# Layer 1 attention: the last key blocks of two query sets transposed together in every second slot, and the adjacency diagonal treated on GpSimd

## The chip, the cores and the metric

The kernel runs on one core of one Trainium2 chip. The metric is the device time of one execution in microseconds (us). TensorE is called PE here (its weight loads PEld), VectorE DVE, ScalarE ACT, GpSimd POOL, and SyncE, which issues the transfers, SP. All data is float32.

## The reference

Two graph layers over 4096 nodes with 512 features, each behind a layer norm and a Relu, each added to its input. The change touches the second layer alone:

```python
# --- layer 1 ---
h = jnp.maximum(_layernorm(x, axis=-1), 0.0)
adj = jnp.maximum(adjacency, jnp.eye(4096))          # 4096 x 4096
keys    = jnp.einsum('nj,hjk->hnk', h, Wks)          # 8 heads of 64
queries = jnp.einsum('nj,hjk->hnk', h, Wqs)
values  = jnp.einsum('nj,hjk->hnk', h, Wvs)
atts = jnp.einsum('hqk,hmk->hqm', queries, keys) / 8
atts = atts - 1e16 * (1.0 - adj)[None, :, :]
atts = softmax(atts, axis=-1)
x = x + jnp.einsum('hqm,hmk,hko->qo', atts, values, Wo)
```

The adjacency holds zeros, values of up to 1e9, and a diagonal.

## The kernel before, in words

Layer 0 comes first, and writes its output, the queries, keys and values of layer 1 to DRAM. Layer 1 starts about halfway through the span.

Layer 1 works on pairs of heads (`c` = 0 to 3). For each pair it goes through 128 **sets** of 32 query rows. A set is folded so that it fills all partitions: partition quadrant `a` (32 partitions) holds the 32 queries against keys `a*1024` to `a*1024+1023`, so a set is a tile of 128 x 1024 for each of the two heads. Four sets make a group (128 queries). The exponentials live in a ring `t` of 12 sets.

One loop runs over **slots** `s`, one set per slot, 512 slots and a few more. In one slot, sets of different age are at different stages. The order of instructions on every engine is the order of the program text; no scheduler moves them. The stages of a slot, in that order:

- `with_self(s+1)` (L897): for pair 0 alone, DVE takes the maximum of the set's 32x32 diagonal block of the adjacency and the identity. The block is in partition quadrant 0 for sets 0 to 31, quadrant 1 for sets 32 to 63, and so on.
- `keep_penalty(s)` (L906): for pair 0, SP writes the finished penalty to DRAM, from where the pairs 1 to 3 load it again (L886).
- `squares(s-4)` (L973): DVE transposes the first 768 key columns of both heads in blocks of 32x32, in place.
- `turned(s-4)` (L979): PE transposes the last 256 key columns, two 128x128 blocks for each head, into the PSUM tile `tr`.
- `smallest` (L950, L955), in odd slots: a matmul `nmB` and a DVE reduction give the softmax shift `nm` of the two sets `s-3` and `s-2`.
- `scores(s)` (L915) and `masked(s)` (L931): PE multiplies queries and keys into four PSUM tiles `sc` (tiles of 64 rows by 32 columns of the array), and DVE adds the penalty `a` and keeps the minimum, in four pieces.
- `taken(s-4)` (L985): ACT copies `tr` back into `t`.
- `exps(s-3)` (L966): ACT's two exponentials.
- `made_penalty(s+1)` (L901, L902): for pair 0, ACT's Relu on the adjacency tile and POOL's `(a - 1) * -1e16`.
- `parted(s)` (L940), in odd slots: POOL prepares the operand of `nmB`.
- `weighted(s-8)` (L996): PE multiplies values by exponentials (tiles of 128 rows by 64 columns of the array), a quarter of the keys of a whole group in each slot. The last quarter reads what `turned` gave.
- `divided`: now and then a sum over partitions (`tot`, L1011), a reciprocal and a small transpose (`invT`, L1019) for half a pair of heads.
- `prefetch(s+5)`: SP's loads of the adjacency (pair 0: four transfers of 128 KB, L889) or of the penalty (L886).

PSUM has eight banks: `sc` takes four, `tr` one, `nmB`, `tot` and `invT` share two (pool `a1m`), and `o` one.

Of the kernel before, what the change touches and what calls it, by code (L numbers as in the profile page):

```python
# [8 lines left out]
F32 = mybir.dt.float32  # L9
AF = mybir.ActivationFunctionType  # L10
ALU = mybir.AluOpType
AX = mybir.AxisListType
PSUM = bass.MemoryType.PSUM
DRAM = bass.MemoryType.DRAM

P = 128
# [7 lines left out]
def kernel(  # L24
# [14 lines left out]
    nc = tc.nc  # L39
# [14 lines left out]
    ident = const.tile([P, P], F32, name="ident")  # L54
# [5 lines left out]
    SQ = 32  # L60
# [38 lines left out]
    with tc.tile_pool(name="a0k", bufs=1) as pk, tc.tile_pool(name="a0v", bufs=4) as pv, tc.tile_pool(  # L99
        name="a0a", bufs=3  # L100
    ) as pa, tc.tile_pool(name="a0t", bufs=6) as pt, tc.tile_pool(name="a0p", bufs=4) as pp, tc.tile_pool(
        name="a0x", bufs=1
    ) as px, tc.tile_pool(name="a0h", bufs=3) as ph, tc.tile_pool(name="a0s", bufs=4) as psb, tc.tile_pool(
        name="a0tr", bufs=3, space=PSUM
# [68 lines left out]
        def turned(G, i):  # L173

            trs = []
            for b in range(MB):
                if b % 4 == 0:
                    tr = ptr.tile([P, TW], F32, name="tr")
                    trs.append(tr)
                for h in range(2):  # L180
                    nc.tensor.transpose(  # L181
                        tr[:, bass.ts(b % 4 * 2 + h, P)], G.t[h][:, bass.ts(i * MB + b, P)], ident
                    )
            return trs

        def taken(G, i, trs):
            for j, tr in enumerate(trs):
                pT = pp.tile([P, TW], F32, name="pT")
                if tiles_out[0] % 7 in (2, 5):
                    nc.scalar.copy(pT, tr)  # L190
                else:
                    nc.vector.tensor_copy(pT, tr)  # L192
                tiles_out[0] += 1
                G.pT[i, j] = pT
# [230 lines left out]
        def step(n):  # L425
            return groups[n // 2], n % 2

        with tc.manual_schedule():
# [45 lines left out]
            for s in range(total + 6):  # L474
                G, h = step(s) if s < total else (None, 0)
                for half in range(2):
# [4 lines left out]
                    turn = 0 <= n < 2 * total  # L481
# [11 lines left out]
                    if half == 1 and s + 1 < total:  # L493
                        leaky(*step(s + 1))

                        c, at = divmod(s + 3, 2 * NB)
# [11 lines left out]
                    if 1 <= n <= 2 * total:  # L508
                        W, w = groups[(n - 1) // HALVES], (n - 1) % HALVES
# [12 lines left out]
    QK_ = N // NS  # L522
    GS = P // SQ
# [4 lines left out]
    EXPS, TURN, PROD = 3, 4, 8  # L528
    BR = 2
    UNITS = 6  # L530
    with tc.tile_pool(name="b0c", bufs=1) as pc, tc.tile_pool(name="b0a", bufs=4) as pa, tc.tile_pool(
        name="b0w", bufs=1
    ) as pk, tc.tile_pool(name="b0t", bufs=1) as pt, tc.tile_pool(name="b0v", bufs=GS) as pv, tc.tile_pool(
        name="b0x", bufs=6
    ) as pxr, tc.tile_pool(name="b0h", bufs=4) as ph, tc.tile_pool(name="b0e", bufs=4) as pe, tc.tile_pool(
        name="b0ht", bufs=2
    ) as phT, tc.tile_pool(
        name="b0s", bufs=6
    ) as psb, tc.tile_pool(name="b0o", bufs=1) as px, tc.tile_pool(
        name="b0lk", bufs=2, space=PSUM  # L540
    ) as plk, tc.tile_pool(name="b0m", bufs=1, space=PSUM) as pm, tc.tile_pool(
        name="b0po", bufs=1, space=PSUM
    ) as po, tc.tile_pool(name="b0q", bufs=2, space=PSUM) as pmm:
        t = pt.tile([P, RING, 2, QK_], F32, name="bt")
# [101 lines left out]
        def squares(G, k):  # L646
            u = t[:, G.ring + k].rearrange("p h (n j) -> p h n j", j=SQ)
            nc.vector.transpose(u, u)  # L648
# [116 lines left out]
        with tc.manual_schedule():  # L765
# [4 lines left out]
            for s in range(SETS + PROD + 10):  # L770
# [23 lines left out]
                if s % 2 and s < SETS:  # L794
                    G, k = step(s)
# [3 lines left out]
                if s % 2 == 0 and 0 <= s - 2 < SETS:  # L799
                    G, k = step(s - 2)  # L800
# [3 lines left out]
                if 0 <= n < SETS:  # L804
                    W, w = step(n)
# [20 lines left out]
    VC = 768  # L826
    NV = VC // SQ
    NT = (QK_ - VC) // P
    SG = NG // 2
    with tc.tile_pool(name="a1t", bufs=1) as pt, tc.tile_pool(name="a1k", bufs=4) as pkk, tc.tile_pool(  # L830
        name="a1v", bufs=GS
    ) as pv, tc.tile_pool(name="a1a", bufs=6) as pa, tc.tile_pool(name="a1q", bufs=2) as pq, tc.tile_pool(
        name="a1x", bufs=2
    ) as px, tc.tile_pool(name="a1s", bufs=6) as psb, tc.tile_pool(name="a1z", bufs=2) as pz, tc.tile_pool(name="a1at", bufs=3) as pat, tc.tile_pool(
        name="a1sc", bufs=4, space=PSUM
    ) as psc, tc.tile_pool(name="a1tr", bufs=1, space=PSUM) as ptr, tc.tile_pool(
        name="a1m", bufs=2, space=PSUM
    ) as pm, tc.tile_pool(name="a1o", bufs=1, space=PSUM) as po:
        t = pt.tile([P, RING, 2, QK_], F32, name="t")
        sums = pt.tile([P, HC, 2, 2, SG, GS], F32, name="sums")  # L840
# [13 lines left out]
        def load_keys(c):  # L854
            keys[c] = []
            for half in range(2):
                k = pkk.tile([P, NS, HF], F32, name="k")
                nc.sync.dma_start(
                    k, qk_d[:, c, 0, :].rearrange("p (a f x) -> p f a x", a=NS, f=2)[:, half]
                )  # L860
                keys[c].append(k)
# [19 lines left out]
        def penalty(G, k):  # L881

            w = G.g * GS + k
            a = pa.tile([P, QK_], F32, name="a")
            if G.c > 0:
                nc.sync.dma_start(a, pen_d[w])  # L886
                return a
            for b in range(NS):
                nc.sync.dma_start(a[bass.ts(b, SQ)], adj[bass.ts(w, SQ), bass.ts(b, QK_)])  # L889
            return a  # L890

        def with_self(G, k, a):
            if G.c == 0:
                w = G.g * GS + k
                b, at = divmod(w * SQ, QK_)
                diag = a[bass.ts(b, SQ), bass.ds(at, SQ)]
                nc.vector.tensor_max(diag, diag, ident[bass.ts(b, SQ), bass.ts(b, SQ)])  # L897

        def made_penalty(G, k, a):
            if G.c == 0:  # L900
                nc.scalar.activation(a, a, AF.Relu)  # L901
                nc.gpsimd.tensor_scalar(a, a, -1.0, -BIG, ALU.add, ALU.mult)  # L902

        def keep_penalty(G, k, a):
# [68 lines left out]
            nc.vector.transpose(u, u)  # L973

        def turned(G, k):
            tr = ptr.tile([P, 512], F32, name="tr")
            for h in range(2):
                for m in range(NT):
                    nc.tensor.transpose(  # L979
                        tr[:, bass.ts(h * NT + m, P)], t[:, G.ring + k, h, bass.ds(VC + m * P, P)], ident  # L980
                    )
            return tr

        def taken(G, k, tr):
            nc.scalar.copy(t[:, G.ring + k, :, VC:], tr.rearrange("p (h x) -> p h x", h=2))  # L985

        def weighted(G, i):
            if i == 0:
# [102 lines left out]
        def load_queries(i):  # L1091
            q = pq.tile([P, QG * P], F32, name="q")
            c, g = divmod(i * QG, NG)
            nc.sync.dma_start(q, qk_d[:, c, 1, bass.ds(g * P, QG * P)])
            for j in range(QG):
                groups[i * QG + j].q, groups[i * QG + j].q0 = q, j * P
# [4 lines left out]
        with tc.manual_schedule():  # L1101
            pens = {}

            def prefetch(n):
                if n < total:
                    if n % (QG * GS) == 0:
                        load_queries(n // (QG * GS))
                    pens[n] = penalty(*step(n))

            AHEAD = 5  # L1110
            rb = 0
            divisions = []
            load_keys(0)
            for n in range(AHEAD):
                prefetch(n)
            with_self(*step(0), pens[0])
            made_penalty(*step(0), pens[0])
            for i in range(GS):
                load_values(0, i)
            for s in range(total + PROD + 3):  # L1120
                if s + 1 < total:
                    with_self(*step(s + 1), pens[s + 1])
                if s < total:
                    keep_penalty(*step(s), pens[s])

                c, at = divmod(s + 4, SETS)
                if 0 < c < HC and at == 0:
                    load_keys(c)
                c, at = divmod(s - PROD - 1 + GS, SETS)
                if 0 < c < HC and at < GS:  # L1130
                    load_values(c, at)
                turn = 0 <= s - TURN < total
                if turn:
                    squares(*step(s - TURN))
                    tr = turned(*step(s - TURN))

                if s % 2 and 0 <= s - 3 < total:
                    G, k = step(s - 3)
                    smallest(G, k // 2)
                n = s - PROD  # L1140
                if 0 < n <= total and n % GS == 0:
                    finish(groups[n // GS - 1])
                if s > total:
                    projected(rb)
                    rb += 1
                if s < total:
                    scs = scores(*step(s))
                    masked(*step(s), scs, pens.pop(s))
                if turn:
                    taken(*step(s - TURN), tr)  # L1150
                if 0 <= s - EXPS < total:
                    exps(*step(s - EXPS))
                if s + 1 < total:
                    made_penalty(*step(s + 1), pens[s + 1])
                if s % 2 and s < total:
                    G, k = step(s)
                    parted(G, k // 2)
                if 0 <= n < total:
                    W, w = step(n)
                    weighted(W, w)  # L1160
                if n > 1 and n % (SG * GS) == 1:
                    divisions.append(divided(*divmod(n // (SG * GS) - 1, 2)))
                for d in divisions[:1]:
                    if next(d, d) is d:
                        divisions.pop(0)
                if s == (HC - 1) * SETS + SETS // 2:
                    wot = pkk.tile([P, HC, DM], F32, tag="k", name="wot")
                    nc.sync.dma_start(wot, wo.rearrange("h d o -> (h d) o").rearrange("(c p) o -> p c o", p=P))
                if s > total - AHEAD and len(chunks) < 3:
                    load_chunk()  # L1170
                prefetch(s + AHEAD)

            for j in range(rb, NB):
                projected(j)
# [28 lines left out]
```

## Time and profile before

| | us |
|---|---|
| median of three runs | 4974.71 (4970.81 to 4975.93) |
| the profiled execution | 4974.76 |
| its span, first to last instruction | 4973.0 |
| L915 PE scores, 16384 instructions | busy 1004.0 |
| L996 PE weighted sums, 16384 | busy 1008.3 |
| L979 PE transposes, 2048 | busy 348.5 |
| L931 DVE masked pieces, 2048 | busy 1291.3 |
| L973 DVE block transposes, 512 | busy 907.7 |
| L966 ACT exponentials, 1024 | busy 1168.0 |
| L985 ACT copies of `tr`, 512 | busy 298.9 |

The span is the profiler's first to last instruction of one execution; the execution's own time is a little more. Busy times of a line add up the time in which at least one of its instructions ran. In listings by time the columns are the start, the length, the engine and line, the operation, what it writes and reads, the shapes, the count, and in brackets how long the engine had been idle before and what released it. A matmul of the program counts as two instructions there for `sc`, `o` and `nmB`, and as one for a transpose. The ends of matmuls are modelled, so two rows of PE can overlap by some hundredths of a us; the chain of waits cuts such overlaps away.

### The profile page before, as it was taken

Reading aid. Unit: us, or ns where it says so; the run is one execution under the profiler, and the core shown is the slowest. Engines: PE = TensorE matmul, PEld = TensorE weight load, DVE = VectorE, ACT = ScalarE, POOL = GpSimd, SP = SyncE. Lnnn points to the kernel's source line nnn. Section 1 sums busy time; section 2 is a strip of 40 time slices with the busy share of each in tenths; the row PEclk is TensorE's granted clock in tenths of the full one; section 3 lists DMA queues with packets and bytes.
Section 4 is the critical chain, followed back from the end, with each engine's and each line's share of the span. In section 5 each row is a group of like instructions: output and inputs, shape, how many; then the busy total and the mean of one; then the engine's idle time right before and its main releaser. Section 6 shows DMA issues by size and latency. Waiting matters only on the chain.

```text
span 4973.0 us, 145263 instructions
## 1 busy us (share of the span) xinstructions
PE 4747.3 (95%) x61554; PEld 3507.7 (71%) x61554; DVE 4509.1 (91%) x7969; ACT 3912.2 (79%) x4557; POOL 396.1 (8%) x676
## 2 busy tenths in 40 slices
PE   6999999999999868998989999999999999999998
PEld 5888888888888756776746656666666666666664
DVE  4999999999999898888659999999999999999981
ACT  4999999999999898888658888666666666666660
POOL 1000000000000011111112222000000000000000
PEclk8999999999999979999999999999999999999999
DMA  6444454445444474444377787634444343533435
GB/s 236 156 150 162 171 183 154 157 154 197 165 147 163 121 170 141 134 143 141 100 217 242 239 261 239 200 129 144 137 160 152 128 153 127 187 128 136 152 121 191
DMA packets 358842, 819.49 MB, mean 165 GB/s; under 512 B 60080, under 2 KB 179120, under 8 KB 333104
## 3 DMA queue, kind: packets, MB, share of 16 engines
q1 hardware_dynamic: 358192, 810.21, 49.8%
q8 instruction: 483, 7.91, 0.7%
q14 instruction: 167, 1.37, 0.1%
HBM read 669.26 MB, written 140.77 MB: 163 GB/s over the span
## 4 chain that ended last, share of the span: by engine, by line
PE 42%; DMA 3%; issue 2%; SPq 1%; ACT 1%; DVE 1%; POOL 0%; ACTq 0%; POOLq 0%; DVEq 0%
PE sc L915 17%; PE o L996 17%; PE tr L979 5%; PE oo L1079 2%; DMA a<-in_adj_dram 2%; ACT t L966 1%; PE nmB L950 1%; SPq L889 1%; POOL a L902 0%; DVE t L931 0%; PE mp L727 0%; DMA z<-inv_d 0%; PE mpv L739 0%; DMA att_d<-z 0%; DMA v<-v_d 0%
## 5 line engine op out<-in xcount | busy, mean ns | idle before, releaser
L931 DVE CUSTOM_DVE_ANT_0 t<-sc,a 128x512 f32<-128x512 f32 x2048 | 1291.3, 686 | 70.8 <-issue 41.2
L966 ACT ACTIVATE t<-t,nm 128x1024 f32<-128x1024 f32 x1024 | 1168.0, 1143 | 177.3 <-DVE nm L955 177.3
L996 PEld LDWEIGHTS o<-t,v 128*64 128x64 f32 x16384 | 884.6, 137 | 428.7 <-issue 363.1
L915 PE MATMUL sc<-k,q 64*32 64x512 f32 x16384 | 1004.0, 597 | 10.6 <-DVE nm L931 10.5
L996 PE MATMUL o<-t,v 128*64 128x128 f32 x16384 | 1008.3, 276 | 0.0
L973 DVE STREAM_TRANSPOSE t<-t 128x1536 f32<-128x1536 f32 x512 | 907.7, 1773 | 5.0 <-ACT t L966 2.0
L158 DVE CUSTOM_DVE_ANT_0 t<-t,a 128x2048 f32<-128x2048 f32 x384 | 877.0, 2284 | 38.8 <-ACT t L147 38.7
L181 PE MATMUL tr<-ident,t 128*128 128x128 f32 x6144 | 781.4, 278 | 34.0 <-ACT pT L190 20.1
L203 PE MATMUL o<-pT,v 128*64 128x128 f32 x12288 | 756.9, 276 | 1.1 <-DVE pT L192 1.0
L181 PEld LDWEIGHTS tr<-ident,t 128*128 128x128 f32 x6144 | 665.4, 141 | 125.8 <-issue 65.3
L147 ACT ACTIVATE t<-tb,src 128x4096 f32<-128x4096 f32 x192 | 731.6, 3811 | 16.8 <-DMA tb<-trg_d 16.8
L168 ACT ACTIVATE t<-t,nm 128x4096 f32<-128x4096 f32 x192 | 731.2, 3808 | 8.6 <-DVE nm L163 8.5
L203 PEld LDWEIGHTS o<-pT,v 128*64 128x64 f32 x12288 | 664.1, 137 | 61.4 <-issue 47.4
L192 DVE COPY pT<-tr 128x1024 f32<-128x1024 f32 x549 | 653.6, 1216 | 9.8 <-PE tr L181 9.8
L985 ACT COPY t<-tr 128x512 f32<-128x512 f32 x512 | 298.9, 584 | 445.6 <-PE tr L979 441.8
L915 PEld LDWEIGHTS sc<-k,q 64*32 64x32 f32 x16384 | 251.3, 106 | 351.6 <-issue 314.4
L979 PE MATMUL tr<-ident,t 128*128 128x128 f32 x2048 | 348.5, 288 | 11.6 <-ACT t L966 8.4
L599 ACT ACTIVATE lk<-tb,srcb 128x1024 f32<-128x1024 f32 x256 | 282.3, 1113 | 82.3 <-DVE nm L609 75.2
L609 DVE CUSTOM_DVE_ANT_0 bt<-lk,ba 128x1024 f32<-128x1024 f32 x256 | 301.9, 1215 | 24.8 <-ACT e L733 12.7
L648 DVE STREAM_TRANSPOSE bt<-bt 128x2048 f32<-128x2048 f32 x128 | 295.1, 2306 | 28.9 <-ACT bt L641 28.9
L979 PEld LDWEIGHTS tr<-ident,t 128*128 128x128 f32 x2048 | 213.9, 141 | 116.1 <-issue 83.1
L641 ACT ACTIVATE bt<-bt,nm 128x1024 f32<-128x1024 f32 x256 | 290.3, 1135 | 0.4 <-DVE nm L630 0.3
(115 smaller groups left out, 3781.7 us busy)
## 6 DMA issues: line engine op xcount, KB each, us to landing
a<-in_adj_dram SPq DMA_DIRECT2D x192, 1024.0 KB
a<-pen_d SPq DMA_DIRECT2D x384, 512.0 KB
ba<-in_adj_dram SPq DMA_DIRECT2D x512, 128.0 KB
a<-in_adj_dram SPq DMA_DIRECT2D x512, 128.0 KB
pen_d<-a SPq DMA_DIRECT2D x128, 512.0 KB
h<-hT_d SPq DMA_DIRECT2D x96, 256.0 KB
qk_d<-e SPq DMA_DIRECT2D x64, 256.0 KB
x<-in_x_dram SPq DMA_DIRECT2D x8, 1024.0 KB
```

Of the source, the lines that this page charges most:

```text
L147: nc.scalar.activation(t, targets[G.c, h], AF.Prelu, bias=src[:, G.g, 2 * G.c + h : 2 * G.c + h + 1], alpha=SLOPE)
L158: nc.vector.tensor_tensor_reduce(out=t, in0=t, in1=rows_of_adj[G, f], scale=-1.0, scalar=FMAX, op0=ALU.add, op1=ALU.min, accum_out=nm[:, f ...
L168: nc.scalar.activation(G.t[h], G.t[h], AF.Exp, bias=G.nm[h][:, NCH : NCH + 1], scale=-1.0, accum_out=G.sm[:, h : h + 1],)
L181: nc.tensor.transpose(tr[:, bass.ts(b % 4 * 2 + h, P)], G.t[h][:, bass.ts(i * MB + b, P)], ident)
L192: nc.vector.tensor_copy(pT, tr)
L203: nc.tensor.matmul(G.o[h * D : (h + 1) * D, :P], lhsT=feats[G.c][i][:, b, bass.ts(h, D)], rhs=pT[:, bass.ts(b % 4 * 2 + h, P)], start=(mb ...
L915: nc.tensor.matmul(sc[h][bass.ts(a, SQ), :], lhsT=G.q[bass.ts(h, D), bass.ds(G.q0 + k * SQ, SQ)], rhs=keys[G.c][half][bass.ts(h, D), a, :] ...
L931: nc.vector.tensor_tensor_reduce(out=t[:, G.ring + k, h, cols], in0=scs[half][h], in1=a[:, cols], scale=1.0, scalar=FMAX, op0=ALU.add, op1 ...
L966: nc.scalar.activation(u, u, AF.Exp, bias=G.nm[k // 2][:, k % 2, h : h + 1], scale=-1.0, accum_out=G.sm[:, h, k : k + 1],)
L973: nc.vector.transpose(u, u)
L979: nc.tensor.transpose(tr[:, bass.ts(h * NT + m, P)], t[:, G.ring + k, h, bass.ds(VC + m * P, P)], ident)
L996: nc.tensor.matmul(G.o[bass.ts(h, D), :P], lhsT=v[:, b, bass.ts(h, D)], rhs=t[:, bass.ds(G.ring, GS), h, bass.ds(at, SQ)], start=(mb == 0) ...
```

## The change

- `turned` is called in odd slots alone and transposes the last blocks of two sets, `s-5` and `s-4`, eight blocks in a row. Even slots have no transposes on PE. `squares` stays in every slot.
- `tr` grows from 128x512 (one PSUM bank) to 128x1024 (two banks), in one buffer as before. To make room, the pool of `nmB`, `tot` and `invT` goes from two buffers to one.
- `taken` copies both sets at once, in odd slots: one ACT copy of 128x1024 for two of 128x512.
- In pair 0, DVE's maximum with the identity is gone. POOL subtracts the identity from the diagonal block before ACT's Relu, and adds it after it: `relu(a - 1) + 1` is `max(a, 1)`. The rest of the penalty is as before.

```diff
-        name="a1m", bufs=2, space=PSUM
+        name="a1m", bufs=1, space=PSUM
...
-        def with_self(G, k, a):
+        def on_self(G, k, a, op):
+            w = G.g * GS + k
+            b, at = divmod(w * SQ, QK_)
+            diag = a[bass.ts(b, SQ), bass.ds(at, SQ)]
+            nc.gpsimd.tensor_tensor(diag, diag, ident[bass.ts(b, SQ), bass.ts(b, SQ)], op)
+
+        def without_self(G, k, a):
             if G.c == 0:
-                w = G.g * GS + k
-                b, at = divmod(w * SQ, QK_)
-                diag = a[bass.ts(b, SQ), bass.ds(at, SQ)]
-                nc.vector.tensor_max(diag, diag, ident[bass.ts(b, SQ), bass.ts(b, SQ)])
+                on_self(G, k, a, ALU.subtract)
 
         def made_penalty(G, k, a):
+
             if G.c == 0:
                 nc.scalar.activation(a, a, AF.Relu)
+                on_self(G, k, a, ALU.add)
                 nc.gpsimd.tensor_scalar(a, a, -1.0, -BIG, ALU.add, ALU.mult)
...
         def turned(G, k):
-            tr = ptr.tile([P, 512], F32, name="tr")
-            for h in range(2):
-                for m in range(NT):
-                    nc.tensor.transpose(
-                        tr[:, bass.ts(h * NT + m, P)], t[:, G.ring + k, h, bass.ds(VC + m * P, P)], ident
-                    )
+
+            tr = ptr.tile([P, 2, 2, NT * P], F32, name="tr")
+            for j in range(2):
+                for h in range(2):
+                    for m in range(NT):
+                        nc.tensor.transpose(
+                            tr[:, j, h, bass.ts(m, P)],
+                            t[:, G.ring + k - 1 + j, h, bass.ds(VC + m * P, P)], ident,
+                        )
             return tr
 
         def taken(G, k, tr):
-            nc.scalar.copy(t[:, G.ring + k, :, VC:], tr.rearrange("p (h x) -> p h x", h=2))
+            nc.scalar.copy(t[:, bass.ds(G.ring + k - 1, 2), :, VC:], tr)
...
                 turn = 0 <= s - TURN < total
                 if turn:
                     squares(*step(s - TURN))
+                turn = turn and (s - TURN) % 2
+                if turn:
                     tr = turned(*step(s - TURN))
```

The two calls of `with_self` become calls of `without_self`.

More of the change, by code (lines that the diff above doesn't have):

```diff
@@ L1115 @@
                 prefetch(n)
-            with_self(*step(0), pens[0])
+            without_self(*step(0), pens[0])
             made_penalty(*step(0), pens[0])
@@ L1121 @@
                 if s + 1 < total:
-                    with_self(*step(s + 1), pens[s + 1])
+                    without_self(*step(s + 1), pens[s + 1])
                 if s < total:
```

## The prediction

> **What bounds the kernel now.** The page first: its busy shares don't say enough.
>
> ```profile
> PE 4747.3 (95%) x61554; PEld 3507.7 (71%) x61554; DVE 4509.1 (91%) x7969; ACT 3912.2 (79%) x4557; POOL 396.1 (8%) x676
> ```
>
> Three engines are near full, so I read layer 1 by stretches (busy time by window; after the window's length come PE, PEld, DVE, ACT, POOL, then PE clock, DMA share, GB/s).
>
> ```profile
> 3000.00:3050.00 50.00, 49.57 (x757) 30.01 (x756) 49.05 (x116) 42.54 (x71) 12.73 (x17) 1.00 0.74 237
> 4000.00:4500.00 500.00, 499.98 (x7780) 312.18 (x7766) 480.42 (x1072) 335.30 (x594) 23.37 (x64) 1.00 0.45 149
> ```
>
> Head pairs 1 to 3 (3114 to 4823 us) have PE busy without a gap. Pair 0 (2527 to 3114) has small PE gaps and DVE at 98%. The chain of waits in the later pairs holds PE alone (start, us, what):
>
> ```profile
> 4016.30 0.42 PE tot L1011 x2
> 4016.72 0.44 PE tr L979 x4
> ...
> 4030.20 0.59 PE tr L979 x4
> 4030.79 0.14 PE nmB L950 x2
> 4030.93 1.88 PE sc L915 x32
> 4032.81 1.90 PE o L996 x32
> 4034.71 0.59 PE tr L979 x4
> 4035.29 1.88 PE sc L915 x32
> 4037.17 1.90 PE o L996 x32
> ```
>
> Two slots take 2x0.59 + 0.14 + 2x1.88 + 2x1.90 = 8.88 us. The first two lines give a price: the same four transposes take 0.44 behind tot, a full-array matmul like them, and 0.59 behind o. So the step from o's 128x64 tiles to the full array costs about 0.16. Likewise sc streams 4 rounds of 0.43 (the pitch of its weight loads in the timeline), 1.71 of its 1.88, and o 32 loads in 1.73 of 1.90: each change of tile shape costs 0.16 to 0.19, and two slots hold six (o-tr, nmB-sc, sc-o, o-tr, tr-sc, sc-o).
>
> In pair 0 the timeline shows a ring of work that closes every two slots:
>
> ```profile
> 2803.61 0.15 DVE L955 TENSOR_REDUCE nm<-nmB 128x4 f32<-128x32 f32 x1
> 2803.80 1.15 ACT L966 ACTIVATE t<-t,nm 128x1024 f32<-128x1024 f32 x1 [1.25 <-DVE nm L955]
> ...
> 2806.08 1.04 ACT L901 ACTIVATE a<-a 128x1024 f32<-128x1024 f32 x1
> ...
> 2807.20 1.05 POOL L902 TENSOR_SCALAR a<-a 128x1024 f32<-128x1024 f32 x1 [4.41 <-ACT a L901]
> ...
> 2808.28 0.69 DVE L931 CUSTOM_DVE_ANT_0 t<-sc,a 128x512 f32<-128x512 f32 x1
> ...
> 2810.85 0.18 DVE L897 TENSOR_TENSOR a<-a,ident 32x32 f32<-32x32 f32 x1
> ...
> 2811.06 1.78 DVE L973 STREAM_TRANSPOSE t<-t 128x1536 f32<-128x1536 f32 x1
> ...
> 2812.76 0.15 DVE L955 TENSOR_REDUCE nm<-nmB 128x4 f32<-128x32 f32 x1
> ```
>
> From minimum to next minimum: 0.19 to the exponentials, 2.28 for two, 1.12 Relu, 1.08 POOL, 2.57 four masked pieces, 0.21 max, 1.70 squares = 9.15 us. DVE is all but full within it as well. Before 2680 us the same ring measures 8.90 (2604.04 to 2612.94), just at PE's 8.88: there max starts as soon as the masked piece allows and squares follow 0.11 later; after 2680, from set 32 on, whose diagonal lies on partitions 32 and up, max comes 0.12 late and holds squares for 0.21.
>
> **What the Trainium skill says.** "TensorEngine Tiling (Array Packing)", Key Properties: changing the tiling mode drains TensorE. The 0.44 against 0.59 agrees. "VectorE: DVE Perf Modes", section Two Vector instructions with no wait between them: an instruction whose start quadrant differs from the last one's is held until all before it are done. The step at set 32 agrees: 0.33 per max where it was 0.11. "GPSIMD Engine Reference", Instruction dispatch: a POOL instruction that reads what the one before wrote needs a wait on its completion. The changed program has it (the penalty waits for POOL's own semaphore); no run here shows its price.
>
> **The change part by part.**
>
> *Transposes (both sets of a pair in odd slots).* As many transposes, but 8 in a row in odd slots and none in even ones. Layer 0 has 8 in a row behind the same o: 1.09 us in the timeline, where 4 show 0.66 there; the slope is 0.11 each. In the chain that is 0.59 + 4x0.11 = 1.03 in place of 1.18: **-0.15 to -0.16 a pair of slots**. The even slot has o-sc in place of o-tr and tr-sc. No o-sc is in the trace. I take it at 0.17, since all four kinds seen cost 0.16 to 0.19; then five changes are left of six. Bounds: 0 (saves 0.33) and 0.33 (saves nothing). Pairs 1 to 3 hold 192 pairs of slots (1540 transposes between 3114 and 4823, eight a pair): **-31 us**, from 0 to -63.
>
> Does anything take PE's place there? DVE without max needs 2x(1.70 + 4x0.61) + 0.08 = 8.4 to 8.5 against PE's 8.72: it follows, with 0.2 to spare. ScalarE's copy (L985) goes from two of 0.58 to one of 128x1024, about 1.0 (L190, the same shape out of PSUM, shows 0.98); it stands in front of the odd slot's exponentials. With PE's odd slot as zero: transposes done at 1.03, copy 1.1 to 2.1, exponentials (minimum ready about 2.1) to 4.5, and squares, which need them, come up at 4.8 behind the masked pieces. Just covered by 0.2 to 0.3; if late, DVE's spare takes it. The next transposes need the even slot's exponentials, done near 7, at 8.72.
>
> *PSUM.* tr takes two banks in one buffer: the next transposes come 8.7 us later, the copy ends 6 us before. a1m falls to one buffer: nmB is read by DVE within the slot; tot and invT (eight times each) fall in an odd and the next even slot, and the reciprocal (0.94) or the small copy behind them ends before the next nmB, over which eight transposes lie. Cost 0; without that cover some 1 us each, 8 us at most.
>
> *Diagonal in pair 0.* DVE loses 128 max (0.18, with holds 0.33 each from set 32). POOL gains two 32x32 ops a set. The subtract waits for the adjacency DMA where DVE's max did; behind it on POOL stand that slot's add, penalty and parts, on ScalarE the Relu, then the next copy and exponentials. The rows land some 3.4 us after issue and are asked for about four slots ahead: covered. In the steady state the subtract runs while Relu's turn is over 1 us away: nothing. The add stands in the ring, between Relu and penalty. Nearest row: parts (L940), 128x32 with two inputs, 0.24; with the wait on its own semaphore I take 0.31. Bounds 0.17 (DVE's time for this shape, no wait) and 0.7. The ring becomes 9.15 - 0.33 + 0.31 = 9.13 after set 32, and 8.90 - 0.11 + 0.31 = 9.10 before. Against pitches of 9.15 and 8.88: 47 x -0.02 + 12 x +0.22 = **+1 to +2 us**; PE's saving is hidden there, since the ring sets the pace. With the bounds: -6 to +25. SP's write of the penalty (L906) waits 0.3 longer; the loads queued behind it have slots to spare.
>
> *Start of layer 1.* At 2551.24 max waits 9.28 us for set 5's rows, and squares and masked of set 4 queue behind it. With that wait on POOL they run while DVE would idle; set 5's masked pieces then start after subtract, Relu, add and penalty, near 2554, not 2557.3: **-3 us** (0 to -4).
>
> Sum: -31 - 3 + 1 = -33. The profiled execution took 4974.76 (span 4973.0), the median is 4974.71, so both give **4941 us**.
>
> **Rivals.**
> 1. *The shape change o-sc is nearly free.* sc's small loads could slip in behind o. Against: the drain at every other change. Saves 0.33 a pair: 4974.7 - 63 - 2 = 4910.
> 2. *o-sc costs what two changes did*, or the odd slot's later minimum stalls exponentials and PE stays at 8.88. Against: 0.2 us of cover. Only the start is left: 4972, no change.
> 3. *Slower: POOL's add becomes pair 0's pace.* ScalarE's Relu, then add, then a drained wait, then penalty, in series in each ring. For it: POOL had the last word in the ring already (penalty ends 2808.25, masked starts 2808.28). It outweighs the rest when add and wait exceed about 1.05 us: (33 + 10)/59 pairs = 0.73 above my 0.31. At 1.1 us: 4989. Against: the 0.24 row.
> 4. *The change does not reach PE's order.* Excluded: the changed program has eight transposes in a row in odd slots, sc straight behind o in even ones.
>
> **How the numbers follow.** A measurement of this kernel can tell about 0.2% (10 us) from no change. Main case 70%, range 4924 to 4957 (drain 0.10 to 0.24, ring 9.0 to 9.3); rival 1 12%, rival 2 12%, rival 3 6%. Faster 0.86 (main, rival 1 and a third of the values near rival 2), same 0.08, slower 0.06. The range runs from 4914 (most of rival 1's side, not its end) to 4962 (part of rival 2).
>
> **What would show it.** Right: the chain in pairs 1 to 3 still PE alone, 8 transposes in 1.03, sc in even slots at about 1.88, two slots in 8.72; pair 0 at 9.1 with the add in the ring, the step at set 32 gone; DVE free of L897. Wrong: sc or o behind o-sc longer or shorter by 0.1; PE gaps ahead of sc or tr in pairs 1 to 3; the add with its wait far from 0.3; the start no earlier.

## The result, and the profile after

| | us |
|---|---|
| before, median of 4 | 4972.76 (4970.74 to 4975.93) |
| after, median of 4 | 4939.98 (4939.67 to 4942.85) |
| ratio | 0.9933, 95% interval 0.9921 to 0.9945 |
| the profiled execution after | 4940.09, span 4938.3 |

The change saves 33 us, 0.67%. The prediction was 4941 us. First the page's busy line of the kernel after:

```profile
PE 4719.5 (96%) x61554; PEld 3518.5 (71%) x61554; DVE 4462.5 (90%) x7841; ACT 3857.6 (78%) x4301; POOL 459.2 (9%) x932
```

DVE has 128 instructions fewer, ACT 256 fewer, POOL 256 more and PE as many as before, 28 us shorter. The chain of waits of the kernel after, in the same place as the one shown of before (start, us, what):

```profile
4028.14 1.02 PE tr L986 x8
4029.17 0.14 PE nmB L955 x2
4029.31 1.88 PE sc L920 x32
4031.19 1.90 PE o L1004 x32
4033.09 1.88 PE sc L920 x32
4034.96 1.90 PE o L1004 x32
4036.86 1.02 PE tr L986 x8
```

Eight transposes take 1.02, and sc straight behind o takes the same 1.88 as behind a full-array matmul. Two slots go from 8.87 to 8.72 us, and from 3115 to 4789 us the chain is still PE alone. Pair 0's ring after, from the timeline:

```profile
2811.62 0.15 DVE L960 TENSOR_REDUCE nm<-nmB 128x4 f32<-128x32 f32 x1
2811.81 1.15 ACT L971 ACTIVATE t<-t,nm 128x1024 f32<-128x1024 f32 x1 [1.53 <-DVE nm L960]
...
2814.09 1.04 ACT L905 ACTIVATE a<-a 128x1024 f32<-128x1024 f32 x1
...
2815.21 0.24 POOL L896 TENSOR_TENSOR a<-a,ident 32x32 f32<-32x32 f32 x1 [4.07 <-ACT a L905]
2815.54 1.05 POOL L907 TENSOR_SCALAR a<-a 128x1024 f32<-128x1024 f32 x1
...
2816.62 0.69 DVE L936 CUSTOM_DVE_ANT_0 t<-sc,a 128x512 f32<-128x512 f32 x1 [0.62 <-DMA a<-in_adj_dram]
...
2819.07 1.77 DVE L978 STREAM_TRANSPOSE t<-t 128x1536 f32<-128x1536 f32 x1
...
2820.77 0.15 DVE L960 TENSOR_REDUCE nm<-nmB 128x4 f32<-128x32 f32 x1
```

The ring still takes 9.15 us. DVE now waits 0.62 us in it; the bracket names the DMA, but the penalty on POOL ends at 2816.59, so that is what the masked piece waited for. From the add's start to the penalty's start are 0.33 us: 0.24 of work and a gap of 0.09 in which the penalty waits for the add to be done. DVE gave up 0.33 for the one maximum that stood in the ring from set 32 on, and the add puts 0.33 in its place.

The softmax shift (`nm`) is reduced once every two slots, so its start times cut layer 1 into 256 steps. From the two timelines:

| step | before, us | after, us | after - before |
|---|---|---|---|
| first sc (start of layer 1) | 2527.01 | 2528.87 | +1.86 |
| 5 | 2586.23 | 2582.95 | -3.28 |
| 14 | 2666.37 | 2665.26 | -1.11 |
| 36 | 2867.66 | 2866.52 | -1.14 |
| 37 | 2878.51 | 2875.67 | -2.84 |
| 62 | 3107.41 | 3104.45 | -2.96 |
| 255 | 4822.26 | 4789.50 | -32.76 |
| end of the span | 4973.0 | 4938.3 | -34.7 |

In this pair of executions layer 0, which the change does not touch, was 1.9 us longer. The start of layer 1 gained 5.1, steps 5 to 14 lost 2.2, the one step of the first division gained 1.7, the later pairs gained 29.8 over 193 steps, and the end 1.9. In the kernel before, that division step reads:

```profile
2870.30 0.95 DVE L1016 RECIPROCAL inv<-tot 32x128 f32<-32x128 f32 x1
...
2871.25 1.04 POOL L902 TENSOR_SCALAR a<-a 128x1024 f32<-128x1024 f32 x1 [4.25 <-DMA a<-in_adj_dram]
2871.27 1.06 DVE L897 TENSOR_TENSOR a<-a,ident 32x32 f32<-32x32 f32 x1
```

The reciprocal makes the maximum late, so that it starts just after POOL's penalty and takes 1.06 us in place of 0.18. After the change DVE has no maximum to be late with, and its spare time takes in the reciprocal. The experiments come back to such held maxima.

### The profile page after: what moved, and what is told of

The parts are those of the page before. It is cut to its first block, busy times and chain, and to the rows that moved or that the text cites. A ratio compares the mean times of both kernels' runs of the same rounds, so it can differ in the third digit from the quotient of the medians.

```text
span 4938.3 us, 144474 instructions
## 1 busy us (share of the span) xinstructions
PE 4719.5 (96%) x61554; PEld 3518.5 (71%) x61554; DVE 4462.5 (90%) x7841; ACT 3857.6 (78%) x4301; POOL 459.2 (9%) x932
## 4 chain that ended last, share of the span: by engine, by line
PE 57%; ACT 15%; DVE 15%; issue 8%; DMA 3%; SPq 1%; POOL 0%; DVEq 0%; ACTq 0%; POOLq 0%
PE sc L920 20%; PE o L1004 20%; ACT t L168 6%; PE tr L986 5%; DVE t L158 5%; DVE pT L192 4%; ACT t L147 4%; DVE bt L609 3%; PE tr L181 3%; PE o L203 3%; ACT pT L190 2%; PE oo L1087 2%; ACT bt L641 2%; DVE bt L648 2%; DMA ba<-in_adj_dram 1%
## 5 line engine op out<-in xcount | busy, mean ns | idle before, releaser
L920 PE MATMUL sc<-k,q 64*32 64x512 f32 x16384 | 1028.1, 597 | 10.5 <-DVE nm L936 10.4
L181 PE MATMUL tr<-ident,t 128*128 128x128 f32 x6144 | 781.5, 278 | 34.1 <-ACT pT L190 20.1
L181 PEld LDWEIGHTS tr<-ident,t 128*128 128x128 f32 x6144 | 665.4, 141 | 125.9 <-issue 65.3
L993 ACT COPY t<-tr 128x1024 f32<-128x1024 f32 x256 | 259.1, 1012 | 515.9 <-PE tr L986 507.0
L656 PE MATMUL bo<-bt,bv 128*64 128x128 f32 x4096 | 282.8, 297 | 5.9 <-ACT boT L665 4.5
L986 PE MATMUL tr<-ident,t 128*128 128x128 f32 x2048 | 280.8, 280 | 0.8 <-ACT t L971 0.7
```

Source lines behind the costliest of these rows:

```text
L181: nc.tensor.transpose(tr[:, bass.ts(b % 4 * 2 + h, P)], G.t[h][:, bass.ts(i * MB + b, P)], ident)
L920: nc.tensor.matmul(sc[h][bass.ts(a, SQ), :], lhsT=G.q[bass.ts(h, D), bass.ds(G.q0 + k * SQ, SQ)], rhs=keys[G.c][half][bass.ts(h, D), a, :] ...
L986: nc.tensor.transpose(tr[:, j, h, bass.ts(m, P)], t[:, G.ring + k - 1 + j, h, bass.ds(VC + m * P, P)], ident,)
```

## The experiments

Three questions: is it PE's order that pays in the later pairs; what sets pair 0's pace; and do the two halves of the change stand alone? The pitch is the median time between two `nm` reductions, two slots; where two values alternate, both stand.

| kernel | pitch, sets 12 to 27 | sets 32 to 123 | pairs 1 to 3 | time, us | its before, us |
|---|---|---|---|---|---|
| before | 8.90 | 9.15 | 8.87 | 4972.76 | |
| after | 9.14 | 9.15 | 8.72 | 4939.98 | 4972.76 |
| transposes alone | 9.50 and 9.66 | 9.62 and 9.78 | 8.72 | 4971.94 | 4972.73 |
| POOL's diagonal alone | 9.14 | 9.15 | 8.87 | 4973.37 | 4972.73 |
| PE's order as before | 9.14 | 9.15 | 8.87 | 4968.04 | 4972.73 |
| two copies | 9.14 | 9.15 | 8.72 | 4939.05 | 4972.73 |
| no add | 8.82 | 8.82 | 8.72 | 4922.57 | 4975.24 |
| two more in the ring | 9.78 | 9.80 | 8.72 | 4979.27 | 4975.24 |
| maximum in quadrant 0 | 8.91 | 8.91 | 8.87 | 4961.8 | 4975.24 |
| penalty two ahead | 8.71 | 8.72 | 8.72 | 4924.97 | 4975.24 |
| transposes, one input | 8.90 | 9.18 | 8.72 | 4942.25 | 4975.27 |
| two ahead from slot 12 | 8.72 | 8.72 | 8.72 | 4923.43 | 4975.27 |
| the same, seven buffers | 8.71 | 8.72 | 8.72 | 4919.28 | 4975.27 |

Before, after, the first two-ahead kernel and the last two are medians of several executions; the others are one execution each. Executions of the kernel before range from 4970.74 to 4977.05 us, so a difference of a few us between single executions says nothing; the pitches do. The kernels "no add", "maximum in quadrant 0" and "transposes, one input" leave the true diagonal out of the penalty; they are there for their time alone.

### PE's order or ScalarE's copy

The changed kernel with PE's order of before; the copy stays merged:

```diff
-                turn = turn and (s - TURN) % 2
-                if turn:
...
+            if k % 2 == 0:
+                pair_tr[0] = ptr.tile([P, 2, 2, NT * P], F32, name="tr")
...
+                        tr[:, k % 2, h, bass.ts(m, P)],
+                        t[:, G.ring + k, h, bass.ds(VC + m * P, P)], ident,
...
+            if k % 2:
+                nc.scalar.copy(t[:, bass.ds(G.ring + k - 1, 2), :, VC:], tr)
```

> The changed kernel, but PE transposes each set's last blocks in that set's own slot, as before, into the two halves of the two-bank tile; ScalarE's copy stays one of 128x1024 in odd slots, and PSUM and POOL are as in the changed kernel. Theory: the order on PE is what pays, so pairs 1 to 3 go back to 8.87 us for two slots: 4970 us. Rival (the merged copy or the freed ScalarE pays): 8.71 us, 4940 us.

Its chain in the later pairs:

```profile
4002.44 1.90 PE o L1007 x32
4004.34 0.59 PE tr L988 x4
4004.92 1.88 PE sc L920 x32
```

4968.04 us, and 8.87 for two slots: with the four transposes back in the even slot the whole gain of pairs 1 to 3 is gone, though the copy is merged. The reverse, PE's order as changed and the copy split:

```diff
-            nc.scalar.copy(t[:, bass.ds(G.ring + k - 1, 2), :, VC:], tr)
+            for j in range(2):
+                nc.scalar.copy(t[:, G.ring + k - 1 + j, :, VC:], tr[:, j])
```

> The changed kernel, with two copies of 128x512 on ScalarE in odd slots in place of one of 128x1024. Theory: ScalarE has spare, so pairs 1 to 3 stay at 8.71 us for two slots although the copies take 1.17 in place of 1.01 and the exponentials may start some 0.1 later: 4940 us. Rival (the merged copy pays): up to 0.16 a pair of slots lost, 4970 us.

4939.05 us and 8.72: the merged copy, 0.16 us of ScalarE for each two slots, is worth nothing here. Both rivals fall.

That it is the number of shape changes that counts, and not eight transposes in a row as such, shows at the divisions. There a full-array `tot` stands between o and sc in the even slot:

```profile
3997.63 0.42 PE tot L1019 x2
3998.05 1.88 PE sc L920 x32
3999.92 1.90 PE o L1004 x32
4001.82 0.17 PE invT L1027
4001.99 1.02 PE tr L986 x8
```

The same work in the kernel before, from `tot` at 4016.30 (shown in the prediction) to the end of the odd slot's transposes at 4021.69, takes 5.39 us; here it takes 5.38. Where `tot` brings the shape change back, putting the transposes together saves nothing.

### What sets pair 0's pace

POOL's add left out:

```diff
                 nc.scalar.activation(a, a, AF.Relu)
-                on_self(G, k, a, ALU.add)
```

> The changed kernel without POOL's add behind the Relu (the diagonal of the penalty is then not the reference's; the subtract stays). Theory: the add stands in pair 0's ring with 0.33 us, so pair 0 goes from 9.15 to about 8.82 us for two slots, 60 pairs of slots: 20 us, to 4920 us. Rival (POOL is hidden there and something else sets 9.15): pitch 9.15, 4940 us.

8.82 us and 4922.57: as expected, the add, which this kernel leaves out, costs 0.33 us in every two slots of pair 0. Two more of its kind:

```diff
                 on_self(G, k, a, ALU.add)
+                on_self(G, k, a, ALU.subtract)
+                on_self(G, k, a, ALU.add)
```

> The changed kernel with a second subtract and a third add behind the Relu in pair 0. Theory: every such operation with its wait adds 0.33 us to the ring, so two slots take 9.15 + 0.66 = 9.81 us in pair 0 and the total rises by about 40 us to 4980 us. Rival (POOL's time is hidden): 4940 us.

Its timeline, from the first of the three to the masked piece behind them:

```profile
2803.05 0.89 POOL L896 TENSOR_TENSOR a<-a,ident 32x32 f32<-32x32 f32 x3 [3.73 <-ACT a L905]
2804.03 1.05 POOL L909 TENSOR_SCALAR a<-a 128x1024 f32<-128x1024 f32 x1
...
2805.11 0.69 DVE L938 CUSTOM_DVE_ANT_0 t<-sc,a 128x512 f32<-128x512 f32 x1 [1.27 <-POOL a L909]
```

9.80 us, 0.325 for each of the two, and 4979.27: DVE, whose work is the same, waits 1.27 us in place of 0.62. The ring goes up and down with POOL's small operations one for one. The rival that POOL is hidden falls.

The last test opens the ring: the penalty is made for the set two slots ahead.

```diff
+            without_self(*step(1), pens[1])
+            made_penalty(*step(1), pens[1])
...
-                if s + 1 < total:
-                    without_self(*step(s + 1), pens[s + 1])
+                if s + 2 < total:
+                    without_self(*step(s + 2), pens[s + 2])
```

and the same for `made_penalty` in the slot.

> The changed kernel, with the subtract, Relu, add and penalty of pair 0 for the set two slots ahead in place of one. Theory: the ring is opened, since the masked pieces no longer wait for a penalty made in the same slot; pair 0 then runs at PE's 8.71 us for two slots in place of 9.15: 60 x 0.44 = 26 us, about 4914 us (ratio to before 0.988). Rival (transfers, ScalarE's load of about 8.0 us, or another wait sets pair 0's pace): pitch between 8.8 and 9.15, 4920 to 4940 us.

Pair 0 runs at PE's 8.72, as the theory has it, but the time is 4924.97 (ratio to before 0.9896, interval 0.9880 to 0.9913), 11 us over the forecast. The steps show where: the fifth `nm` starts at 2589.45, 6.5 us later than in the changed kernel (its first sc starts 4.1 later already), and of the steps near 2900 us, behind the first division, two take 12.9 and 9.4 us. There the adjacency rows are late, since they are needed one slot sooner than before:

```profile
2904.78 1.06 ACT L905 ACTIVATE a<-a 128x1024 f32<-128x1024 f32 x1 [4.43 <-DMA a<-in_adj_dram]
...
2907.25 2.50 POOL L1052 TENSOR_TENSOR z<-z 128x512 f32<-128x512 f32 x2
...
2909.84 0.24 POOL L896 TENSOR_TENSOR a<-a,ident 32x32 f32<-32x32 f32 x1
2910.11 1.06 ACT L905 ACTIVATE a<-a 128x1024 f32<-128x1024 f32 x1 [1.11 <-POOL a L896]
```

Behind the late rows stands a second cost: POOL scales the finished outputs of the division (`z`, L1052) in front of its next subtract, and ScalarE's Relu waits for that subtract. So two more kernels: one ahead until slot 12, then two; and the same with seven buffers, loads six ahead.

```diff
+                lead = 1 if s < 12 else 2
...
-        name="a1a", bufs=6
+        name="a1a", bufs=7
...
-            AHEAD = 5
+            AHEAD = 6
```

> The changed kernel with pair 0's penalty made two sets ahead, from slot 12 on; before that one ahead, so that the start is not delayed. Theory: 7 us of start come back against the kernel that is two ahead from the first slot, about 4918 us. Rival (the start is bound by the transfers either way): 4925 us.

> The same with seven adjacency buffers and loads six sets ahead. Theory: with two ahead a late adjacency transfer (around the divisions, some 4 us near 2904 us) reaches PE; one more buffer hides it: about 4914 us. Rival (the transfers come at the same time whatever is asked earlier): as without it, 4918 us, or later at the start by one more load.

Both missed their numbers. The first took 4923.43 (0.9896, 0.9881 to 0.9911). The fifth `nm` is back at 2583.99, but stepping from one to two ahead costs a step of 11.4 and the division steps take 15.2 and 9.4 in the profiled execution. With seven buffers the step at slot 12 still takes 10.6, the division steps take 9.8 and 8.7, and the time is 4919.28 (4918.89 to 4920.43; 0.9888, 0.9871 to 0.9904), 5 us over its forecast. In the step of 9.8 Relu waits 2.04 us for the subtract behind POOL's `z`, which one more buffer does not move. Even so this is the fastest kernel of the study, 20.7 us under the changed one.

### The two halves alone

The changed kernel with DVE's maximum of before (transposes alone; POOL's add goes too), and the kernel before with POOL's diagonal. The first edit:

```diff
-                on_self(G, k, a, ALU.subtract)
+                nc.vector.tensor_max(diag, diag, ident[bass.ts(b, SQ), bass.ts(b, SQ)])
```

> The changed kernel, with VectorE's maximum of the kernel before in place of POOL's two operations. Theory (one change of tile shape less per two slots pays in pairs 1 to 3; pair 0 follows its ring): pairs 1 to 3 at 8.71 us for two slots, pair 0 as before (8.90 up to set 32, then 9.15), the start as before; about 4941 us. Rival (VectorE's relief from the maximum brought the gain): pitch near 8.87, about 4970 us.

> The kernel before, with the diagonal on POOL as in the changed kernel. Theory: pairs 1 to 3 stay at 8.87 us for two slots; pair 0 at 9.15 for all sets (up to set 32 slower than the 8.90 of before, then equal); the first sets of layer 1 some 5 us earlier; the sum near zero, 4970 us. Rival (VectorE's relief brought the gain): about 4945 us.

POOL's diagonal alone did what was expected: nothing in sum. The transposes alone did not: the later pairs run at 8.72, yet the time is 4971.94, since pair 0 slows to 9.70 on average from set 32 on. Neither the theory nor the rival had that. Its timeline:

```profile
2804.30 1.04 POOL L902 TENSOR_SCALAR a<-a 128x1024 f32<-128x1024 f32 x1 [2.12 <-ACT a L901]
...
2804.57 0.80 DVE L897 TENSOR_TENSOR a<-a,ident 32x32 f32<-32x32 f32 x1
...
2805.41 1.78 DVE L973 STREAM_TRANSPOSE t<-t 128x1536 f32<-128x1536 f32 x1
...
2807.11 0.15 DVE L955 TENSOR_REDUCE nm<-nmB 128x4 f32<-128x32 f32 x1
...
2813.92 1.04 POOL L902 TENSOR_SCALAR a<-a 128x1024 f32<-128x1024 f32 x1 [1.95 <-ACT a L901]
...
2814.36 0.64 DVE L897 TENSOR_TENSOR a<-a,ident 32x32 f32<-32x32 f32 x1
```

The odd slot's maximum, 0.18 us in the kernel before, takes 0.80 and 0.64 in turn here. The first ends at 2805.37, just behind POOL's penalty (2805.34). In the kernel before, the even slot's ScalarE copy kept Relu, and so POOL's penalty, to 7.45 us after `nm` (2811.06 against 2803.61), and the maximum started ahead of it, at 7.24 (2810.85). Without that copy the penalty starts 6.81 after `nm` (2813.92 against 2807.11), and the maximum, at 7.25, runs into it. The Trainium skill's "GPSIMD Engine Reference", Specifications, says that POOL's SBUF interfaces are shared with VectorE and contended by VectorE instructions with two SBUF inputs; the maximum has two. A test, against the transposes alone: an operation of one input in the same place, the maximum left out.

```diff
-                nc.vector.tensor_max(diag, diag, ident[bass.ts(b, SQ), bass.ts(b, SQ)])
+                nc.vector.transpose(diag, diag)
```

> The kernel with the transposes alone, but VectorE's maximum of the diagonal block with the identity (two inputs in SBUF) is replaced by a transpose of that block in place (one input; the penalty's diagonal is then not the reference's). Theory: in the transposes-alone kernel the maximum falls into POOL's penalty operation and lasts until that ends[...]; with one input it is not held up, pair 0 goes from 9.7 to about 9.15 us for two slots (8.9 before set 32), total about 4940 us. Rival (the odd slot's eight transposes or ScalarE's longer copy slow pair 0's ring): pitch stays near 9.7, 4972 us.

```profile
2800.79 1.04 POOL L902 TENSOR_SCALAR a<-a 128x1024 f32<-128x1024 f32 x1 [1.97 <-ACT a L901]
2801.22 0.20 DVE L897 STREAM_TRANSPOSE a<-a 32x32 f32<-32x32 f32 x1
```

It falls into POOL's penalty as well and takes 0.20; pair 0 is at 9.18 (8.90 up to set 32) and the time is 4942.25. So neither the eight transposes nor the long copy slows pair 0; the held maximum does, with some 30 us. That the two inputs are the reason agrees with the skill, but is not shown alone: the test changes the kind of operation (a transpose for a maximum) together with the number of inputs. The runs show that this operation of one input, of the same size in the same place, is not held.

### The step at set 32

```diff
-                b, at = divmod(w * SQ, QK_)
+                b, at = 0, w * SQ % QK_
```

in the kernel before.

> The kernel before, with VectorE's maximum of every set on partitions 0 to 31 (from set 32 on that is not the diagonal). Theory (an instruction that starts in another quadrant than its neighbours is held): no step at set 32, pair 0 at 8.90 us for two slots throughout, 47 x 0.25 = 12 us less than before: 4961 us. Rival (the step at set 32 comes from something else that starts then, such as the transfers): 9.15 us from set 32 on, 4973 us.

8.91 us in both stretches and 4961.8: with the maximum always on partitions 0 to 31 there is no step at set 32.

## Why the prediction was right

- **Pairs 1 to 3, -31.** Measured -29.8 from step 62 to 255, 0.15 for two slots, and none where a division's `tot` stands in the even slot. The step that carried it, the unseen o-sc taken at the price of the four changes seen, held: sc takes 1.88 behind o as behind tr. Eight transposes were put at 1.03 and take 1.02.
- **Nothing takes PE's place there.** Held: PE is busy without a gap. The copy was put at 1.0 and takes 1.01; splitting it changed nothing.
- **PSUM.** No wait for tr's single buffer or for a1m shows in the chain. Smaller pools alone were not tried.
- **Pair 0, +1 to +2.** The ring was put at 9.13 and 9.10 and takes 9.15 and 9.14; the add with its wait was put at 0.31 and measures 0.33. Steps 5 to 14 lost 2.2 and the late steps nothing, but for the 1.7 gained at the division. That POOL's work stands in the ring, and DVE's relief brings no speed there, was right; the two runs that took an operation from POOL or added some show it.
- **Start, -3 (0 to -4).** It gained 5.1 against the first sc: too small by 2, and outside its own bounds. The set after the late rows came earlier, as worked out: its masked pieces start at 2556.40, 27.5 us after the first sc, where before they started 30.3 after it (2557.34). The rest came later. Of it, 0.84 is one held maximum: in the kernel before, the one at 2564.59 takes 1.02 us beside POOL's penalty. Some 1.5 is not explained. The collision was in the trace of the kernel before, here and at 2871.27, and I had not read it.
- **Rivals.** The cheap and the dear o-sc fell by the chain. POOL's add as a new pace was the right mechanism with a harmless size: 0.33 against the 1.05 from which it would have decided.
- **What the sum did not see, and luck.** The two halves were summed as if each stood alone, and pair 0 was taken to keep its ring whatever the transposes do. The total came out, the halves don't: neither the transposes alone nor POOL's diagonal alone differs from the kernel before by more than its executions do among themselves (4971.94 and 4973.37), and together they gain 33. The diagonal's move is worth some 30 us, for it takes away a collision that the other half makes. That the two were changed together, so that the collision the prediction never weighed could not arise, was luck. So, in part, is a total within 1 us: the start gained 2 more than forecast, the later pairs 1 less, the end 1.9 that stood in no sum, and layer 0 was 1.9 longer in the profiled pair.

## What to carry to other kernels

Count changes of tile shape in a PE-bound loop: here each costs 0.15 to 0.17 us, and two small full-array groups put together save one. Where a stage runs at the pace of a ring, follow it across the engines before crediting relief on one of them; to open it, make its operand a slot earlier, with a buffer more, and look at what else stands in that engine's order (here POOL's `z`). And when an instruction is moved, look at what it now runs beside: a short operation can be held by a long one of another engine.

## What was not expected of the hardware

- A VectorE operation of 32x32 with two inputs in SBUF, begun while POOL worked on a 128x1024 tile, ended only when POOL's did, 0.03 to 0.04 us behind it, in all 63 cases of three kernels with more than 0.3 us of POOL's work left (2 before, 59 with the transposes alone, 2 with the maximum in quadrant 0): 0.64 to 1.06 us in place of 0.17 to 0.19. Where POOL began while the maximum ran, 27 times in the kernel before, neither was longer.
- A 32x32 maximum costs DVE 0.33 us when it starts in another partition quadrant than its neighbours and 0.11 when it does not; the last experiment above takes the step away. The prediction had this from the trace; the size is what these runs add.
- A dependent POOL operation costs 0.33 us in series, of which 0.24 is work and 0.09 the gap before the operation that reads it.
